# Fetching an adjacency matrix in pairs of row blocks: 4 MB transfers in place of 2 MB ones, and larger x transfers

## The chip, the cores and the metric

The kernel runs on one core of a Trainium2 chip. The metric is the device time of one execution in microseconds. Before the change the median of three runs is 235.88 us (235.42 to 236.04).

## What is computed

One layer of a graph attention network, a residual and a layer norm. The reference, cut to what matters:

```python
ht  = (x @ W).reshape(N, 4, 512).transpose(1, 0, 2)        # x: 4096 x 512, W: 512 x 2048
src = einsum('hnd,hd->hn', ht, a[:, :512, 0]); dst = einsum('hnd,hd->hn', ht, a[:, 512:, 0])
e   = leaky_relu(src[:, :, None] + dst[:, None, :], 0.01) + adj[None]   # adj: 4096 x 4096
att = softmax(e, axis=-1)
y   = einsum('hij,hjd->hid', att, ht).mean(axis=0)
out = layernorm(x + y, axis=-1)
```

The entries of `adj` are 0 or of the order of up to 1e9. In such a row the softmax is one-hot at the largest entry of the row of `adj`, as long as the gap to the second largest is big enough. The kernel relies on this: it finds the column of the largest entry of each row, gathers that row of x, multiplies it by the mean of W over the heads, adds x and normalises. A bound on the attention scores tells whether a row's gap is big enough; a general path behind a branch serves rows for which it isn't. With these inputs the branch isn't taken.

## The kernel before

Partition p of the 128 holds rows 32p to 32p + 31 of x, adj and the output. Block ib (0 to 31) is row 32p + ib of every partition: 128 rows of adj, 16 KB each, 2 MB in all. So for one partition the rows of block ib and ib + 1 lie next to each other in memory. All of x (8 MB) passes through one tile `hold` of 32 slots of 512 columns; the 4 MB of W lie in its slots 16 to 31 at first, until they are used up, and the results are written over x.

One loop over t = 0 to 31 (from L423 on) records the instructions of all engines; each engine then runs its own instructions in that order. In step t:

- **SP** issues all plain transfers, in order: first x, if `x_at` has an entry for t (four blocks each, for blocks 4 to 23, issued at t = 3, 7, 11, 15 and 19), then adj of block t + 5 (`load_adj`, L117). `adj_pool` has six buffers, so the transfer of block ib waits until block ib - 6 has been read. Transfers that SP and ACT issue share eight completion semaphores in turn, so a transfer also waits for the one eight before it.
- **DVE** reduces block t in two halves to the maximum of each segment of its row (L169; segments of 16 columns up to block 17, of 32 from 18 on). Between the halves it handles block t - 2: the second largest entry in the leading segment (L208) and the place of the largest (L214), for which that segment (`lead`) must have been gathered. After the halves it finds the eight largest segments (L176) and their index (L178). At t = 16 come the norms of the attention vectors (`head_norms`, L363): DVE copies and squares `pv`, PE multiplies by ones (L368, tile `px`), DVE and ACT finish.
- **POOL** adds the first index (L185) and gathers the leading segment of block t (L191), and for block t - 2 the column (L216) and then the row of x (L202, tile `y`, four buffers). Every second step it also computes the reciprocal deviations of two blocks (`rstd`, L270) from sums that ACT has made.
- **PE** transposes a head of W (L350, t = 1 to 14), transposes y of block t - 3 (`turn`, L229), adds x by an identity matmul (L237), makes the attention vectors (L358, t = 1 to 14) and multiplies y by the mean of W (`products`, L244).
- **ACT** copies the transposes (L352, L231), takes sums of block t - 4 (L266, L268), the squares of x (L251), and finishes two blocks every second step (L277).

Blocks 28 to 30 arrive in two transfers each and block 31 in four (`pieces`, L114), so that DVE can start on a part. Block 0 has four as well. The results of blocks 24 to 27 wait in a buffer of `adj_pool` (`put_by`, L253). After the loop come the stores, the column search in the whole row of block 31 (L222), its gather, its products in two halves (L286) and the last store.

Of the kernel before, what the change touches and what calls it, by code (L numbers as in the profile page):

```python
# [9 lines left out]
F32 = mybir.dt.float32  # L10
# [10 lines left out]
P = 128  # L21
# [47 lines left out]
def leading_rows(ctx, tc, x, adj, W, a, out, ident, v, n_bad, any_bad):  # L69
# [8 lines left out]
    nc = tc.nc  # L78
    N, D = x.shape
    H = a.shape[0]  # L80
    KB, NB, S = D // P, N // P, N // E
    S_EARLY = N // E_EARLY
    AHEAD = 5
    Q = 4
    PIECES = 4
    LATE = NB - Q
    BEHIND = LATE - Q

    once = ctx.enter_context(tc.tile_pool(name="once", bufs=1))
    adj_pool = ctx.enter_context(tc.tile_pool(name="adj_pool", bufs=AHEAD + 1))  # L90
    y_pool = ctx.enter_context(tc.tile_pool(name="y_pool", bufs=4))
    lead_pool = ctx.enter_context(tc.tile_pool(name="lead_pool", bufs=2 * Q + 1))
    small = ctx.enter_context(tc.tile_pool(name="small", bufs=5))
    rows = ctx.enter_context(tc.tile_pool(name="rows", bufs=2))
    psum = ctx.enter_context(tc.tile_pool(name="psum", bufs=4, space=bass.MemoryType.PSUM))

    adj_rows = adj.rearrange("(p nb) m -> nb p m", nb=NB)
    adj_segs = adj.rearrange("n (s e) -> (n s) e", e=E)
    adj_segs_early = adj.rearrange("n (s e) -> (n s) e", e=E_EARLY)
    x_rows = x.rearrange("(p nb) d -> p nb d", nb=NB)  # L100
# [7 lines left out]
    w_sum = once.tile([P, KB, D], F32, name="w_sum")  # L108
    a_rows = once.tile([2 * H, D], F32, name="a_rows")

    once.tile([P, 32], F32, name="pad_end")
    adj_t = {}

    def pieces(ib):  # L114
        return PIECES if ib in (0, NB - 1) else 2 if ib >= LATE else 1

    def load_adj(ib):  # L117
        if 0 <= ib < NB:
            t = adj_t[ib] = adj_pool.tile([P, N], F32, name="adj_t")
            n = pieces(ib)  # L120
            for k in range(n):
                nc.sync.dma_start(t[:, ts(k, N // n)], adj_rows[ib][:, ts(k, N // n)])

    def load_x(lo, n):
        nc.sync.dma_start(hold[:, ds(lo, n), :], x_rows[:, ds(lo, n), :])
# [7 lines left out]
    for kb in range(KB):  # L133
        load_w(kb)
        load_adj(kb + 1)
    load_x(0, Q)
    for ib in range(KB + 1, AHEAD):
        load_adj(ib)

    make_identity(nc, ident)  # L140
    first = once.tile([P, NB], U32, name="first")
# [18 lines left out]
    seg_of, at_of, lead_of, y_t, yt_of, o_ps = {}, {}, {}, {}, {}, {}  # L160

    def segment_maxima(ib, lo, hi):

        e = E_EARLY if ib < EARLY else E
        if lo == 0:
            seg_of[ib] = small.tile([P, N // e], F32, name=f"seg{e}", bufs=2)
        n = max(pieces(ib), 2)
        for k in range(lo * n // PIECES, hi * n // PIECES):
            nc.vector.tensor_reduce(  # L169
                seg_of[ib][:, ts(k, N // e // n)],  # L170
                adj_t[ib][:, ts(k, N // n)].rearrange("p (s e) -> p s e", e=e), axis=AX.X, op=OP.max,
            )

    def find_segment(ib):
        seg = seg_of.pop(ib)
        nc.vector.max(out=top[:, ib, :], in_=seg)  # L176
        at = at_of[ib] = small.tile([P, 8], U32, name="at")
        nc.vector.max_index(at, top[:, ib, :], seg)  # L178
        if ib < NB - 1:
            fetch_segment(ib)  # L180
# [29 lines left out]
    def find_column(ib):  # L210
        if ib < BEHIND:
            find_inner(ib)
        within = small.tile([P, 8], U32, name="within")
        nc.vector.max_index(within, top[:, ib, :], lead_of[ib])  # L214
        col = small.tile([P, 1], U32, name="col")
        nc.gpsimd.tensor_tensor(col, at_of.pop(ib), within[:, 0:1], op=OP.add)  # L216
        gather_rows(ib, col)
# [15 lines left out]
    def residual(ib):  # L233
        start = ib not in o_ps
        if start:
            o_ps[ib] = psum.tile([P, D], F32, name="o")
        nc.tensor.matmul(o_ps[ib], ident, hold[:, ib, :], start=start, stop=False)  # L237
# [11 lines left out]
    def row_norm(ib):  # L249
        sq = rows.tile([P, D], F32, name="sq")  # L250
        nc.scalar.activation(sq, hold[:, ib, :], AF.Square, accum_out=xx[:, ib : ib + 1])  # L251

    def put_by(ib):  # L253

        if ib == BEHIND:
            o_ps["by"] = adj_pool.tile([P, N // D, D], F32, name="adj_t")
        nc.scalar.copy(o_ps["by"][:, ib - BEHIND, :], o_ps.pop(ib))

    def add_x(engine, ib):
# [10 lines left out]
    def rstd(i):  # L270
        nc.gpsimd.tensor_scalar(sd[:, i], sd[:, i], 1.0 / D, EPS, op0=OP.mult, op1=OP.add)
        nc.gpsimd.tensor_tensor(sd[:, i], sd[:, i], power[:, : i.stop - i.start], op=OP.pow)  # L272
        nc.gpsimd.tensor_mul(nm[:, i], nm[:, i], sd[:, i])
# [57 lines left out]
    def mean_of_heads(kb):  # L331
        o = psum.tile([P, D], F32, name="o")
        for h in range(H):
            nc.tensor.matmul(o, ident, hold[:, w_at + kb * H + h, :], start=(h == 0), stop=(h == H - 1))  # L334
        nc.scalar.activation(w_sum[:, kb, :], o, AF.Copy, scale=1.0 / H)  # L335
# [5 lines left out]
    def turn_a():  # L341
        tp = psum.tile([P, KB, P], F32, name="tp", bufs=2)
        for k in range(KB):
            nc.tensor.transpose(tp[:, k, : 2 * H], a_rows[:, ts(k, P)], ident[: 2 * H, : 2 * H])
        nc.scalar.copy(at_d, tp[:, :, : 2 * H])

    def turn_w(kb, h):
        tp = psum.tile([P, KB, P], F32, name="tp", bufs=2)
        for k in range(KB):
            nc.tensor.transpose(tp[:, k, :], hold[:, w_at + kb * H + h, ts(k, P)], ident)  # L350
        wt = rows.tile([P, KB, P], F32, name="wt")
        nc.scalar.copy(wt, tp)  # L352
        return wt

    def head_vector(kb, h, wt):

        for k in range(KB):
            nc.tensor.matmul(  # L358
                pv[:, kb, h : 2 * H : H], wt[:, k, :], at_d[:, k, h : 2 * H : H],
                start=(k == 0), stop=(k == KB - 1),  # L360
            )

    def head_norms():  # L363
        nc.vector.tensor_copy(v, pv)
        vv = once.tile([P, KB, 2 * H], F32, name="vv")
        nc.vector.tensor_mul(vv, v, v)
        pn = psum.tile([P, KB, 2 * H], F32, name="px", bufs=1)
        nc.tensor.matmul(pn, ones, vv, start=True, stop=True)  # L368
        n2 = once.tile([P, 2 * H], F32, name="n2")
        nc.vector.tensor_reduce(n2, pn.rearrange("p k c -> p c k"), axis=AX.X, op=OP.add)  # L370
        nc.scalar.activation(n2, n2, AF.Sqrt)
        both = once.tile([P, H], F32, name="both")
        nc.vector.tensor_add(both, n2[:, :H], n2[:, H:])
        nc.vector.tensor_reduce(vn, both, axis=AX.X, op=OP.max)
# [40 lines left out]
        nc.vector.tensor_reduce(total, pg, axis=AX.X, op=OP.add)  # L415
        nc.vector.tensor_scalar(any_bad, total, -1.0, float(N), op0=OP.mult, op1=OP.add)

    x_at = {lo - 1: (lo, Q) for lo in range(Q, BEHIND, Q)}
    vectors = [(kb, h) for kb in range(KB) for h in range(H)]
    vectors_at = {t: 2 if t < 3 else 1 for t in range(1, 15)}  # L420
    COLUMN, PROJECT, STATS, FINISH = 2, 3, 4, 6
# [1 line left out]
    for t in range(NB):  # L423
        if t == NB // 2:
            tc.mark_branch_hint_location("general", engines=HINTED)
        if t in x_at:
            load_x(*x_at[t])
        if t + AHEAD == NB - 1:
            load_x(LATE, Q)
        load_adj(t + AHEAD)  # L430
        middle = 1 if t == NB - 1 else 2
        segment_maxima(t, 0, middle)
        if t >= COLUMN:
            find_column(t - COLUMN)
        segment_maxima(t, middle, PIECES)
        pair = FINISH <= t < BEHIND + FINISH and t % 2 == 0
        if pair:
            rstd(slice(t - FINISH, t - FINISH + 2))
        if t == NB - 1:
            for ib in (BEHIND, BEHIND + 2):  # L440
                load_x(ib, 2)
        find_segment(t)
        if t < 2:
            mean_of_heads(t)
        elif t == 2:
            mean_of_heads(2)
            mean_of_heads(3)
        if t == 0:
            turn_a()
        turned = [(*vectors[0], turn_w(*vectors.pop(0))) for _ in range(vectors_at.get(t, 0))]  # L450
        if t == 16:
            head_norms()
        ib = t - PROJECT
        if t == NB - 1:
            for late in range(LATE, NB):
                row_norm(late)
        if t == NB - 2:
            residual(LATE)
            residual(LATE + 1)
        if ib >= 0:  # L460
            turn(ib)
            if ib > BEHIND:
                products(ib - 1, KB - 1, KB)
            if ib < BEHIND:
                residual(ib)
        for some in turned:
            head_vector(*some)
        if ib >= 0:
            products(ib, 0, KB if ib < BEHIND else KB - 1)
        if t >= BEHIND + STATS:  # L470
            put_by(t - STATS)
        elif t >= STATS:
            stats(t - STATS)
            row_norm(t - STATS)
        if pair:
            finish(t - FINISH)
            finish(t - FINISH + 1)
# [218 lines left out]
```

## Time and profile before

| | before |
|---|---|
| median of three runs | 235.88 us (235.42 to 236.04) |
| the profiled execution, its own time | 236.22 us |
| its span, first to last instruction | 234.7 us |
| mean granted TensorE clock | 0.959 |
| busy: PE, DVE, ACT, POOL | 200.7, 192.2, 111.7, 100.7 us |
| bytes moved | 97.06 MB at a mean of 414 GB/s |
| SP's queue (q1) | 10080 packets, 88.08 MB, 89.0% of the 16 engines' span |
| POOL's queue (q0), the gathers | 3584 packets, 8.77 MB, 9.5% |
| DVE idle in front of L169, waiting for adj | 29.4 us in 15 waits |

The 40 digits of an engine's row are its busy share in 40 equal slices of the span, in tenths. In a timeline each line has the start and the length in microseconds, the engine, the line of the kernel, the operation with its tiles and shapes, and in brackets the engine's idle time before it and what ended that. A DMA engine moves packets; the trace records the size, the start and the duration of each. What an SP transfer waits for is not idle time of any engine: it matters only if the DMA engines run out of work.

### The profile page before, as it was taken

To read this page: it belongs to the slowest core of one execution; us is meant where nothing else is said; L and a number is where in the kernel's file an instruction comes from. 1 tells how busy PE (TensorE), PEld (TensorE's weight loads), DVE (VectorE), ACT (ScalarE), POOL (GpSimd) and SP (SyncE) were. 2 spreads that over 40 slices of the span, in tenths; PEclk is the share of its full clock that TensorE was granted. 3 is DMA by queue.
4 is the path that set the end of the run, shared out by engine and by line. 5 is a ranking of instruction groups with operands and counts; after the bars stand their busy time and mean duration, and the time that the engine had idled before them with its cause. 6 is when DMAs were issued, how large, how long until landed. Compare 5 with 4: busy or idle time off the path is not lost.

```text
span 234.7 us, 2494 instructions
## 1 busy us (share of the span) xinstructions
PE 200.7 (86%) x683; PEld 103.0 (44%) x683; DVE 192.2 (82%) x302; ACT 111.7 (48%) x267; POOL 100.7 (43%) x212
## 2 busy tenths in 40 slices
PE   0099859999999999999969979789987988999980
PEld 0034514765656555555525424244433442444360
DVE  2726975669969996999689998998699999989871
ACT  2002112255574647474747464646464555187561
POOL 2022142414626463546444555564364554457400
PEclk9999877999999999999997999979997999999998
DMA  6999999999999999999999999999999999999994
GB/s 233 423 409 430 431 429 415 430 426 425 431 431 421 426 428 428 438 418 436 421 437 431 419 434 422 434 417 435 422 436 413 422 426 423 413 425 420 414 374 197
DMA packets 13697, 97.06 MB, mean 414 GB/s; under 512 B 2152, under 2 KB 2664, under 8 KB 7792
## 3 DMA queue, kind: packets, MB, share of 16 engines
q1 hardware_dynamic: 10080, 88.08, 89.0%
q0 software_dynamic: 3584, 8.77, 9.5%
q8 instruction: 6, 0.10, 0.2%
q14 instruction: 11, 0.09, 0.1%
q10 hardware_dynamic: 16, 0.02, 0.0%
HBM read 88.47 MB, written 8.39 MB: 413 GB/s over the span
## 4 chain that ended last, share of the span: by engine, by line
DMA 48%; POOL 19%; issue 17%; DVE 11%; PE 2%; ACT 0%; POOLq 0%; SPq 0%; DVEq 0%
DMA adj_t<-in_adj_dram 42%; DVE seg L169 8%; POOL y L202 6%; POOL lead L191 5%; DMA y<-in_x_dram,col 3%; DMA lead<-in_adj_dram,row 2%; POOL sd L272 2%; PE o L286 2%; DVE col L222 1%; POOL row L185 1%; POOL start L198 1%; POOL col L216 1%; POOL lead_early L191 1%; DVE at L178 1%; DVE top L176 1%
## 5 line engine op out<-in xcount | busy, mean ns | idle before, releaser
L169 DVE TENSOR_REDUCE seg<-adj_t 128x128 f32<-128x2048 f32 (+3 forms) x68 | 145.9, 2148 | 29.5 <-DMA adj_t<-in_adj_dram 29.4
L244 PE MATMUL o<-w_sum,yt 128*128 128x512 f32 x248 | 116.8, 612 | 0.7 <-ACT yt L231 0.7
L244 PEld LDWEIGHTS o<-w_sum,yt 128*128 128x128 f32 x248 | 45.6, 195 | 55.7 <-issue 44.4
L231 ACT COPY yt<-tp 128x512 f32<-128x512 f32 x32 | 18.8, 588 | 44.4 <-PE tp L229 44.3
L202 POOL DMA_INDIRECT y<-in_x_dram,col x32 | 30.9, 964 | 16.5 <-POOL col L216 15.8
L334 PE MATMUL o<-hold,ident 128*128 128x512 f32 x32 | 21.1, 822 | 15.1 <-POOL row L185 11.5
L237 PE MATMUL o<-hold,ident 128*128 128x512 f32 x52 | 29.0, 645 | 0.0
L229 PE MATMUL tp<-ident,y 128*128 128x128 f32 x128 | 20.0, 280 | 9.2 <-DMA y<-in_x_dram,col 9.1
L185 POOL TENSOR_TENSOR row<-at,first 128x1 uint32<-128x1 uint32 x32 | 6.1, 190 | 43.9 <-DVE at L178 43.6
L229 PEld LDWEIGHTS tp<-ident,y 128*128 128x128 f32 x128 | 14.8, 142 | 21.9 <-issue 20.3
L352 ACT COPY wt<-tp 128x512 f32<-128x512 f32 x16 | 9.2, 587 | 31.5 <-PE tp L350 31.5
L191 POOL DMA_INDIRECT lead_early<-in_adj_dram,row x18 | 18.2, 1010 | 8.8 <-POOL row L185 8.8
L216 POOL TENSOR_TENSOR col<-start,within 128x1 uint32<-128x1 uint32 x31 | 5.9, 189 | 36.5 <-DVE within L214 36.5
L251 ACT ACTIVATE sq<-hold 128x512 f32<-128x512 f32 x32 | 19.8, 619 | 0.0
L358 PEld LDWEIGHTS pv<-at_d,wt 128*128 128x128 f32 x128 | 16.3, 191 | 6.8 <-ACT wt L352 3.7
L334 PEld LDWEIGHTS o<-hold,ident 128*128 128x128 f32 x32 | 8.0, 260 | 25.7 <-POOL row L185 11.5
L335 ACT ACTIVATE w_sum<-o 128x512 f32<-128x512 f32 x4 | 2.4, 598 | 33.6 <-PE o L334 33.6
L277 ACT ACTIVATE hold<-o,nm,sd 128x512 f32<-128x512 f32 x24 | 17.2, 771 | 0.0
L191 POOL DMA_INDIRECT lead<-in_adj_dram,row x14 | 14.1, 1006 | 6.9 <-POOL row L185 6.9
L268 ACT ACTIVATE sq<-o,nm 128x512 f32<-128x512 f32 x24 | 16.5, 688 | 0.8
L358 PE MATMUL pv<-at_d,wt 128*128 128x2 f32 x128 | 15.3, 244 | 0.6 <-ACT wt L352 0.6
L266 ACT ACTIVATE sq<-o 128x512 f32<-128x512 f32 x24 | 14.6, 608 | 0.0
(91 smaller groups left out, 151.4 us busy)
## 6 DMA issues: line engine op xcount, KB each, us to landing
adj_t<-in_adj_dram SPq DMA_DIRECT2D x27, 2048.0 KB
hold<-in_x_dram SPq DMA_DIRECT2D x7, 1024.0 KB
adj_t<-in_adj_dram SPq DMA_DIRECT2D x6, 1024.0 KB
out_dram<-hold SPq DMA_DIRECT2D x10, 512.0 KB
adj_t<-in_adj_dram SPq DMA_DIRECT2D x8, 512.0 KB
hold<-in_L_gnn_W_dram SPq DMA_DIRECT2D x4, 1024.0 KB
out_dram<-hold SPq DMA_DIRECT2D x2, 1024.0 KB
hold<-in_x_dram SPq DMA_DIRECT2D x2, 512.0 KB
```

The costliest lines, as they stand in the source:

```text
L169: nc.vector.tensor_reduce(seg_of[ib][:, ts(k, N // e // n)], adj_t[ib][:, ts(k, N // n)].rearrange("p (s e) -> p s e", e=e), axis=AX.X, op ...
L191: nc.gpsimd.indirect_dma_start(out=lead, out_offset=None, in_=adj_segs_early if early else adj_segs, in_offset=bass.IndirectOffsetOnAxis(a ...
L202: nc.gpsimd.indirect_dma_start(out=y, out_offset=None, in_=x, in_offset=bass.IndirectOffsetOnAxis(ap=col[:, :1], axis=0),)
L229: nc.tensor.transpose(tp[:, kb, :], y[:, ts(kb, P)], ident)
L231: nc.scalar.copy(yt, tp)
L237: nc.tensor.matmul(o_ps[ib], ident, hold[:, ib, :], start=start, stop=False)
L244: nc.tensor.matmul(o_ps[ib], yt_of[ib][:, kb, :], w_sum[:, kb, :], start=(start and kb == 0), stop=(kb == KB - 1),)
L251: nc.scalar.activation(sq, hold[:, ib, :], AF.Square, accum_out=xx[:, ib : ib + 1])
L268: nc.scalar.activation(sq, o, AF.Square, bias=nm[:, i], accum_out=sd[:, i])
L277: nc.scalar.activation(hold[:, ib, :], o_ps.pop(ib), AF.Identity, bias=nm[:, i], scale=sd[:, i])
L334: nc.tensor.matmul(o, ident, hold[:, w_at + kb * H + h, :], start=(h == 0), stop=(h == H - 1))
L358: nc.tensor.matmul(pv[:, kb, h : 2 * H : H], wt[:, k, :], at_d[:, k, h : 2 * H : H], start=(k == 0), stop=(k == KB - 1),)
```

## The change

- The six buffers of `adj_pool` become one tile `ring` of six slots; block ib goes to slot ib mod 6.
- Blocks 4 to 15 are fetched two at a time, 32 KB a partition, by `load_pair`. Pair 4, 5 is issued ahead of the loop, behind x of blocks 0 to 3 (before, block 4 was issued ahead of that x and block 5 at t = 0). Pairs 6, 7 to 14, 15 are issued at t = 2, 4, 6, 8 and 10. Since a pair has one completion, its first block can be read when both have landed. A pair is issued when the second of its two slots is free.
- Block 0 comes in one transfer. DVE reduces it in two halves in place of four quarters.
- x of blocks 4 to 11 comes in one transfer at t = 3, and x of blocks 16 to 23 in one at t = 15. Blocks 12 to 15 keep their own at t = 11. So x of blocks 8 to 11 is now issued ahead of adj of blocks 8 to 11, and x of blocks 20 to 23 ahead of adj of blocks 20 to 23; before, each was issued behind them.
- All other instructions of PE, DVE, ACT and POOL, and their order, are the same. SP issues 59 transfers in place of 70.

```diff
+    SLOTS = AHEAD + 1
+    PAIRED = range(4, 16)
...
-    adj_pool = ctx.enter_context(tc.tile_pool(name="adj_pool", bufs=AHEAD + 1))
...
+    adj_pairs = adj.rearrange("(p nb) m -> p nb m", nb=NB)
...
+    ring = once.tile([P, SLOTS, N], F32, name="adj_t")
...
     def pieces(ib):
-        return PIECES if ib in (0, NB - 1) else 2 if ib >= LATE else 1
+        return PIECES if ib == NB - 1 else 2 if ib >= LATE else 1
+
+    def load_pair(ib):
+        slot = ib % SLOTS
+        for k in range(2):
+            adj_t[ib + k] = ring[:, slot + k, :]
+        nc.sync.dma_start(ring[:, ds(slot, 2), :], adj_pairs[:, ds(ib, 2), :])
 
     def load_adj(ib):
-        if 0 <= ib < NB:
-            t = adj_t[ib] = adj_pool.tile([P, N], F32, name="adj_t")
+        if 0 <= ib < NB and ib not in PAIRED:
+            t = adj_t[ib] = ring[:, ib % SLOTS, :]
...
     load_x(0, Q)
-    for ib in range(KB + 1, AHEAD):
-        load_adj(ib)
+    load_pair(PAIRED[0])
...
-            o_ps["by"] = adj_pool.tile([P, N // D, D], F32, name="adj_t")
+            o_ps["by"] = ring[:, (ib + 2) % SLOTS, :].rearrange("p (b d) -> p b d", d=D)
...
-    x_at = {lo - 1: (lo, Q) for lo in range(Q, BEHIND, Q)}
+    x_at = {Q - 1: (Q, 2 * Q), 3 * Q - 1: (3 * Q, Q), 4 * Q - 1: (4 * Q, 2 * Q)}
...
-        load_adj(t + AHEAD)
+        if t + AHEAD in PAIRED[2:]:
+            if t % 2 == 0:
+                load_pair(t + AHEAD - 1)
+        else:
+            load_adj(t + AHEAD)
```

## The prediction

> **What bounds the kernel now.** I read the page's 40 slices first, then the timelines of DVE, PE and POOL. From the page:
>
> ```profile
> DVE  2726975669969996999689998998699999989871
> ...
> DMA  6999999999999999999999999999999999999994
> GB/s 233 423 409 430 431 429 415 430 426 425 431 431 421 426 428 428 438 418 436 421 437 431 419 434 422 434 417 435 422 436 413 422 426 423 413 425 420 414 374 197
> ```
>
> The 16 DMA engines are never idle between 3 and 224 us. More transfers in flight therefore buy nothing. What the change can still give is a lower DMA cost per byte; what it can lose is the date at which a consumer gets its block. DVE is nearly full as well. Its timeline, first reduction of a block, with the idle time before it in brackets (blocks 8, 9, 12, 16, 17, 20, 24, 27, 31):
>
> ```profile
> 67.56 2.29 DVE L169 TENSOR_REDUCE seg<-adj_t 128x128 f32<-128x2048 f32 x1 [1.67 <-DMA adj_t<-in_adj_dram]
> ...
> 73.28 2.29 DVE L169 TENSOR_REDUCE seg<-adj_t 128x128 f32<-128x2048 f32 x1
> ...
> 92.12 2.29 DVE L169 TENSOR_REDUCE seg<-adj_t 128x128 f32<-128x2048 f32 x1 [1.76 <-DMA adj_t<-in_adj_dram]
> ...
> 116.68 2.29 DVE L169 TENSOR_REDUCE seg<-adj_t 128x128 f32<-128x2048 f32 x1 [1.82 <-DMA adj_t<-in_adj_dram]
> ...
> 124.06 2.28 DVE L169 TENSOR_REDUCE seg<-adj_t 128x128 f32<-128x2048 f32 x1
> ...
> 141.37 2.29 DVE L169 TENSOR_REDUCE seg<-adj_t 128x64 f32<-128x2048 f32 x1 [0.78 <-DMA adj_t<-in_adj_dram]
> ...
> 166.18 2.29 DVE L169 TENSOR_REDUCE seg<-adj_t 128x64 f32<-128x2048 f32 x1 [2.56 <-DMA adj_t<-in_adj_dram]
> ...
> 182.84 2.29 DVE L169 TENSOR_REDUCE seg<-adj_t 128x64 f32<-128x2048 f32 x1 [0.30 <-DMA adj_t<-in_adj_dram]
> ```
>
> Two things are to be seen. Without a wait a block costs DVE 5.67 us (segments of 16) or about 5.4 us (segments of 32), and a block arrives every 5.5 us, every fourth one 2.8 us later, behind an x transfer. And after block 8 all of DVE's waits for adj together are 1.76 + 1.82 + 0.78 + 0.07 + 0.16 + 2.56 + 0.30 = 7.45 us. That is all the delay DVE can make good before the end; from block 27 to block 31 (204.20) it runs without a wait, so a delay left there moves the end.
>
> PE is the second full engine. From turn(0) to turn(11) it repeats every 6.06 us with hardly a gap, and the gather of y decides when it may start. POOL's gather of block 6, PE's turn of it, two later turns, and PE's matmul for the head norms:
>
> ```profile
> 70.89 0.97 POOL L202 DMA_INDIRECT y<-in_x_dram,col  x1 [0.54 <-POOL col L216]
> ```
> ```profile
> 79.77 0.63 PE L229 MATMUL tp<-ident,y 128*128 128x128 f32 x4 [0.17 <-DMA y<-in_x_dram,col]
> ```
> ```profile
> 97.98 0.60 PE L229 MATMUL tp<-ident,y 128*128 128x128 f32 x4
> ...
> 104.04 0.60 PE L229 MATMUL tp<-ident,y 128*128 128x128 f32 x4
> ```
> ```profile
> 122.90 0.38 PE L368 MATMUL px<-vv,ones 128*128 128x32 f32 x2 [2.21 <-DVE vv L366]
> ```
>
> At 122.90 PE waits for DVE; if PE came later, DVE would wait for PE, since the next DVE instructions read px.
>
> **The change, part by part.** All sums are made against the profiled execution: 236.22 us, span 234.7, 0.34 above the median of 235.88.
>
> *DMA work removed.* In the trace's packet records one packet of 16384 bytes takes 611 ns, of 8192 309, of 4096 159, of 4 (a completion) 9. So 8192 bytes cost 302 and a packet about 7. The changed transfers are contiguous on both sides. Pairs: 1536 packets of 16 KB become 768 of 32 KB, 768 x 7 / 16 engines = 0.34 us. Block 0: 4 x 159 become 611, 128 rows, 0.20 us. x: 512 packets of 8 KB become 256, 0.11 us. Eleven transfers fewer, each 16 completions: 0.10 us. Together 0.75 us, and 0 at worst. This is all the change can win, and only if the end still follows the landings.
>
> SP issues eleven transfers less (0.33 to 0.45 us each); SP's queue is 7 to 11 MB ahead of the engines until 170 us (bytes issued less bytes in packets that have ended), so this is worth nothing. A pair is issued when its second slot is free, one block later than before: 5.67 us or 2.4 MB off that lead, still over 5 MB. I cost it at nothing; with the lead gone it would be 5 us of idle DMA.
>
> [...]
>
> *Block 0 in one transfer.* DVE began on its first piece at 4.43 and now begins when 2 MB are there, about 8.5; it would end about 13.5 instead of 10.17. Block 1 is waited for until 16.25 (5.12 us of wait), which hides it. The gather of block 0 goes out at about 15 instead of 12.1 and is needed at 26.
>
> *Pairs and the earlier x.* Both blocks of a pair are usable when the second has landed. Block 4 moves from 39.28 to about 48.5 (block 5 was there at 48.80); blocks 4 to 7 then take 4 x 5.67 and end at 71.2. Pair 8, 9: block 8 landed for 67.56, block 9 5.4 us later (73.0; DVE took it unwaited at 73.28), and now x of blocks 8 to 11 (1 MB, 2.7 us) goes ahead of it: 75.7, less 0.3 saved so far, 75.4. So block 8 starts 7.85 us later than before. DVE's remaining slack was 7.45 us. With no further wait DVE would come out 0.4 us late at block 31. Later pairs land before DVE is ready for them (10, 11 at about 86.2 against 86.7); x of blocks 20 to 23 is also early, but DVE is then over 4 us behind.
>
> *The gathers.* This cost is not in the trace of before, since no packet there is over 16 KB. What is there: y gathers that PE waited for took, from issue to PE's turn, 8.88, 8.24, 8.55, 8.43, 7.88 us while the SP queue moved 16 KB packets (blocks 6, 16, 18, 21, 22), and 6.74, 7.69, 7.07, 7.34 near the end, with 4 and 8 KB packets (blocks 26, 27, 29, 31). Medians 8.43 and 7.2: doubling 8 KB to 16 KB costs a gather 1.2 us. Doubling again adds twice as many bytes, 2.4 us. Bounds: 0, if a 32 KB row still moves as 16 KB packets, and 5 x 0.604 = 3.0, if each of the four data packets of an engine and its completion wait for one longer packet. I take 2.4, from the rows.
>
> [...]
>
> Now PE. The gather of block 6 is issued 3.3 us after block 8 starts (67.56 to 70.89): 78.7. turn(6) follows at 78.7 + 8.43 + 2.4 = 89.5 (79.77 before). From there PE has no slack: five periods of 6.06 to turn(11), 5.62 to turn(12) (110.10 to 115.72), 4.8 to the end of its products: PE reaches px at 130.2. DVE, left alone, starts block 16 at 120.9 (75.4 + 49.12 - 3.58 of waits between 67.56 and 116.68) and wants px at 127.1, as 116.68 to 122.90 shows. It must wait 3.1 us. From px to block 17 were 1.16 us, so block 17 starts at 131.4 instead of 124.06, 7.3 late. Slack left after it: 0.78 + 0.07 + 0.16 + 2.56 + 0.30 = 3.87. Block 31 starts about 3.5 us late.
>
> *The tail.* From 204.20 to the end the order is unchanged: the column search, y of block 31 (issued 216.13, PE 223.47), its products, the last store. All of it follows DVE. The gather may be faster, as fewer stores are in flight: 7.34 against the fastest 6.74, so 0 to 0.6; I take 0.2.
>
> Sum: 236.22 + 3.5 - 0.2 = 239.5 profiled; less 0.34, **239.2 us** as a median.
>
> **Rivals.** *The gathers are not slowed* (32 KB moved as 16 KB packets, or the queue not alternating). For it: no trace shows a packet over 16 KB. Against: 4, 8 and 16 KB rows each moved as one packet. Then turn(6) is at 87.1, PE at px at 127.8, block 17 at 129.0, 4.9 late, less 3.87: 1.07 late, 0.2 of it lost in the tail: 237.1 profiled, 236.7 as a median. By DVE alone (block 17 at 120.9 + 7.38 = 128.3) it would be 236.1.
>
> *Faster: the landings decide the end again.* If DVE has caught up by block 27, block 27 lands 0.75 us earlier than 182.84 and everything behind it follows: 235.1. It decides as soon as DVE's delay at block 17 is below 3.1 us (3.87 - 0.75), that is block 17 starts before 127.2. For it: DMA is the chain's largest part, and 7.85 against 7.45 is close. Against: PE alone brings block 17 to 129.0.
>
> *Worse: DVE also waits for leads.* The small gather needs its answer 7.12 us after issue (104.32 to DVE's search at 111.44). With 4 and 8 KB packets it took 5.56 and 5.98 (205.06 to 210.62, 199.73 to 205.71). One data packet and one completion each behind a 32 KB packet would add 2 x 0.9 us: 7.4 to 7.8, a wait of 0.3 to 0.7 in each of blocks 10 to 15. About 3 us of that lie under DVE's wait for px; what is over, and the row gathers that POOL then issues late, would cost 1 to 2 more: 240.2 to 241.4.
>
> **How the numbers follow.** Forecast 0.52 (own range 237.6 to 240.2), gathers not slowed 0.22, faster 0.13, worse 0.13. The range reaches from 235.5 to 241.4; it leaves out most of the faster case and a little at the top. A difference of 0.3% (0.7 us) is about what a measurement of this kernel can tell from no change. Slower by more: forecast, worse, and the upper part of the first rival, 0.71; within: 0.16; faster: 0.13.
>
> **What would show it.** In the changed kernel's trace: packets of 32768 bytes near 1.21 us; block 4 starting near 48.5 and block 8 near 75.4, with a DVE wait before each; PE's turn of block 6 near 89.5 behind a wait for y; no PE idle time before px, and a DVE wait of about 3 us behind it; block 17 near 131.4; no DVE wait for adj after block 8; block 31 near 207.7. Wrong would be: x landing behind pair 8, 9; DVE idle for adj after block 17 (then the delay was made good); gathers no slower between 45 and 107 us; idle DMA engines before 200 us.

## The result, and the profile after

Six runs of the changed kernel have a median of 246.31 us (245.08 to 248.87), six of the kernel before 235.56 (235.36 to 236.04). The ratio of the means is 1.0449 with a 95% interval of 1.0391 to 1.0506; the run at 248.87 us, over 1.5% above the fastest, is left out of it, and the median of the other five is 245.23 us. The profiled execution took 245.21 us with a span of 243.7, at a granted clock of 0.954 (0.959 before). So the change costs about 10 us (10.75 by the medians, 9.0 by the two profiled executions): the direction was forecast, the size was not, and the time lies above the range.

The page of the changed kernel, in the rows that were shown of the kernel before (40 slices, busy share in tenths):

```profile
DVE  0666790199945965679999899999999999989882
DMA  6999999999999999999999999999999999998225
GB/s 247 430 430 418 430 461 427 432 430 432 431 435 422 434 428 427 404 429 432 429 419 431 433 432 416 435 427 424 424 421 424 429 415 424 420 414 339 90 107 201
```

DVE now has a weak stretch from slice 12 to 18 (67 to 110 us: digits 4, 5, 9, 6, 5, 6, 7), and the DMA engines run out of work three slices before the end. The loss was made early; at the end the data were there and the engines were late.

DVE's waits in the changed kernel (waited for; us in total, times, longest):

```profile
DVE seg L177 <- DMA adj_t<-in_adj_dram: 25.6, 5, 11.7
DVE inner L216 <- DMA lead_early<-in_adj_dram,row: 14.2, 5, 3.6
```

The second line is new. Before, the list had only 0.7 us of waiting for a lead, for two late ones (`lead`, L214), and none for `lead_early`. The five waits in DVE's timeline, each with the first reduction of the next block:

```profile
70.75 0.18 DVE L216 MAX8 inner<-lead_early 128x8 f32<-128x16 f32 x1 [3.65 <-DMA lead_early<-in_adj_dram,row]
...
74.64 2.27 DVE L177 TENSOR_REDUCE seg<-adj_t 128x128 f32<-128x2048 f32 x1
...
79.32 0.18 DVE L216 MAX8 inner<-lead_early 128x8 f32<-128x16 f32 x1 [2.41 <-DMA lead_early<-in_adj_dram,row]
...
82.81 2.27 DVE L177 TENSOR_REDUCE seg<-adj_t 128x128 f32<-128x2048 f32 x1
...
87.20 0.18 DVE L216 MAX8 inner<-lead_early 128x8 f32<-128x16 f32 x1 [2.12 <-DMA lead_early<-in_adj_dram,row]
...
90.69 2.27 DVE L177 TENSOR_REDUCE seg<-adj_t 128x128 f32<-128x2048 f32 x1
...
95.55 0.18 DVE L216 MAX8 inner<-lead_early 128x8 f32<-128x16 f32 x1 [2.59 <-DMA lead_early<-in_adj_dram,row]
...
99.03 2.27 DVE L177 TENSOR_REDUCE seg<-adj_t 128x128 f32<-128x2048 f32 x1
...
104.67 0.18 DVE L216 MAX8 inner<-lead_early 128x8 f32<-128x16 f32 x1 [3.37 <-DMA lead_early<-in_adj_dram,row]
...
108.16 2.27 DVE L177 TENSOR_REDUCE seg<-adj_t 128x128 f32<-128x2048 f32 x1
```

Blocks 8 to 12 start at 74.64, 82.81, 90.69, 99.03 and 108.16: 7.9 to 9.1 us apart, where DVE's own work is 5.67. POOL's gathers of this stretch in the changed kernel:

```profile
71.88 0.97 POOL L210 DMA_INDIRECT y<-in_x_dram,col  x1 [0.54 <-POOL col L224]
...
75.92 0.96 POOL L199 DMA_INDIRECT lead_early<-in_adj_dram,row  x1 [0.92 <-POOL row L193]
...
80.45 0.96 POOL L210 DMA_INDIRECT y<-in_x_dram,col  x1 [0.54 <-POOL col L224]
...
83.69 1.07 POOL L199 DMA_INDIRECT lead_early<-in_adj_dram,row  x1 [0.52 <-POOL row L193]
...
88.33 0.96 POOL L210 DMA_INDIRECT y<-in_x_dram,col  x1 [0.54 <-POOL col L224]
...
91.55 0.96 POOL L199 DMA_INDIRECT lead_early<-in_adj_dram,row  x1 [0.51 <-POOL row L193]
```

The lead issued at 75.92 is used at 87.20 (11.3 us), the one issued at 91.55 at 104.67 (13.1 us); 7.12 was what DVE could spare. The y gathers are as late. PE's turns of blocks 5, 6 and 7 in the changed kernel, whose gathers went out at 71.88, 80.45 and 88.33:

```profile
84.83 1.09 PE L237 MATMUL tp<-ident,y 128*128 128x128 f32 x4 [2.26 <-DMA y<-in_x_dram,col]
...
94.41 0.63 PE L237 MATMUL tp<-ident,y 128*128 128x128 f32 x4 [1.73 <-DMA y<-in_x_dram,col]
...
102.31 0.63 PE L237 MATMUL tp<-ident,y 128*128 128x128 f32 x4 [1.65 <-DMA y<-in_x_dram,col]
```

That is 12.95, 13.96 and 13.98 us from issue to use, 8.43 in the median before and 10.83 by the prediction.

The trace's packet records say why. Pairs do move as packets of 32768 bytes: 768, median 1213 ns. POOL's queue carries 3584 packets, 7 for each block on each of the 16 engines (3584 / 32 / 16): four of y, one of the lead and two completions. Between 62 and 102 us it moved 556 of them on 16 engines, 0.87 per engine and microsecond, so one POOL packet in 1.15 us, while SP's queue started 485 large ones: a little over one POOL packet for each. Seven of them take 8.06 us, DVE's new step.

That the step has this length proves nothing by itself, since POOL issues seven packets for each block, however long a block takes. What shows that the queue sets the pace is that it never ran empty: from 62 to 102 us no two of its packets, over all engines, started more than 0.67 us apart. In the kernel before it stood still at four places in the same stretch, for 0.9 to 2.9 us (once from 72.77 to 75.03). Counted in the order of issue, from the first packet's start to the last one's end (gathers issued from 54 to 96 us), a y gather took 3.5 us in the median before and a lead 1.4, together 4.9 of DVE's 5.67; now they take 5.5 and 2.4, together 7.9. So the leads queue up behind the y gathers of earlier blocks.

How it adds up, by starts of blocks on DVE (us):

| | block 4 | 8 | 12 | 17 | 24 | 31 | time |
|---|---|---|---|---|---|---|---|
| before | 39.28 | 67.56 | 92.12 | 124.06 | 166.18 | 204.20 | 236.22 |
| after | 47.91 | 74.64 | 108.16 | 138.16 | 177.05 | 214.65 | 245.21 |

Block 8 is 7.08 us late. From there to block 17 DVE waits 2.41 + 2.12 + 2.59 + 3.37 = 10.49 us for leads and saves the 1.76 + 1.82 = 3.58 us that it waited for adj before: 6.91 more, 14.0 in all, and 14.10 is measured. Of these 3.87 are made good behind block 17 (the slack of the prediction): 10.2, and block 31 is 10.45 late. The tail then takes 1.45 us less (29.05 against 30.5 us from block 31 to the span's end): 9.0, the difference of the two profiled executions. Its last gather is 3.7 us shorter, since the DMA engines are nearly idle by then, but little of that counts: its last packet ended at 229.72 and PE took the rows at 233.18, without a wait, because it was still at the products of earlier blocks. That is 0.74 us sooner after block 31's start than before; the last store gives the other 0.7.

### The profile page after: what moved, and what is told of

Read it like the earlier page. It is cut to its first block, busy times and chain, and to the rows that moved or that the text cites. A ratio compares the mean times of both kernels' runs of the same rounds, so it can differ in the third digit from the quotient of the medians.

```text
span 243.7 us, 2474 instructions
## 1 busy us (share of the span) xinstructions
PE 201.7 (83%) x683; PEld 104.0 (43%) x683; DVE 191.2 (78%) x300; ACT 112.1 (46%) x267; POOL 100.6 (41%) x212
## 3 DMA queue, kind: packets, MB, share of 16 engines
q0 software_dynamic: 3584, 8.77, 9.3%
## 4 chain that ended last, share of the span: by engine, by line
DMA 28%; POOL 23%; issue 23%; PE 19%; DVE 3%; ACT 2%; POOLq 0%; SPq 0%
DMA adj_t<-in_adj_dram 15%; PE o L252 12%; DMA y<-in_x_dram,col 9%; POOL y L210 7%; POOL lead L199 4%; DMA hold<-in_L_gnn_W_dram 4%; POOL lead_early L199 4%; POOL sd L280 3%; PE tp L237 2%; DVE seg L177 2%; PE o L245 2%; POOL start L206 2%; POOL row L193 2%; POOL col L224 2%; PE o L294 1%
## 5 line engine op out<-in xcount | busy, mean ns | idle before, releaser
L177 DVE TENSOR_REDUCE seg<-adj_t 128x128 f32<-128x2048 f32 (+2 forms) x66 | 145.1, 2204 | 25.6 <-DMA adj_t<-in_adj_dram 25.6
L252 PEld LDWEIGHTS o<-w_sum,yt 128*128 128x128 f32 x248 | 44.9, 193 | 54.2 <-issue 44.0
L237 PE MATMUL tp<-ident,y 128*128 128x128 f32 x128 | 20.7, 286 | 20.5 <-DMA y<-in_x_dram,col 20.2
L342 PE MATMUL o<-hold,ident 128*128 128x512 f32 x32 | 20.8, 809 | 14.7 <-DMA hold<-in_L_gnn_W_dram 14.7
L245 PE MATMUL o<-hold,ident 128*128 128x512 f32 x52 | 28.2, 629 | 0.0
L366 PEld LDWEIGHTS pv<-at_d,wt 128*128 128x128 f32 x128 | 17.7, 205 | 7.9 <-issue 4.1
L199 POOL DMA_INDIRECT lead<-in_adj_dram,row x14 | 14.1, 1005 | 6.9 <-POOL row L193 6.6
L366 PE MATMUL pv<-at_d,wt 128*128 128x2 f32 x128 | 16.4, 252 | 0.6 <-ACT wt L360 0.6
## 6 DMA issues: line engine op xcount, KB each, us to landing
adj_t<-in_adj_dram SPq DMA_DIRECT2D x16, 2048.0 KB, 13.9
```

The source lines that it names most:

```text
L177: nc.vector.tensor_reduce(seg_of[ib][:, ts(k, N // e // n)], adj_t[ib][:, ts(k, N // n)].rearrange("p (s e) -> p s e", e=e), axis=AX.X, op ...
L199: nc.gpsimd.indirect_dma_start(out=lead, out_offset=None, in_=adj_segs_early if early else adj_segs, in_offset=bass.IndirectOffsetOnAxis(a ...
L237: nc.tensor.transpose(tp[:, kb, :], y[:, ts(kb, P)], ident)
L252: nc.tensor.matmul(o_ps[ib], yt_of[ib][:, kb, :], w_sum[:, kb, :], start=(start and kb == 0), stop=(kb == KB - 1),)
L366: nc.tensor.matmul(pv[:, kb, h : 2 * H : H], wt[:, k, :], at_d[:, k, h : 2 * H : H], start=(k == 0), stop=(k == KB - 1),)
```

## The experiments

The experiments ask three things: is it the size of the packets, and not the joint completion, the order of x or the ring; does the queue of POOL carry the loss; and is there a version that gains. The theory is that 32 KB packets slow POOL's queue below the rate at which DVE feeds it. Its rivals are the joint landing of a pair, the earlier x, and PE as the bound. Each kernel is compared with the kernel before on the same chip.

### Packets of 16 KB in the same pairs

**e1_apart** moves the slots of the ring 8 elements apart, so that the two rows of a pair are no longer one run in the tile; **e11_apart_512** moves them 128 elements apart. Both keep the pairs, their single completion and all order.

```diff
-    ring = once.tile([P, SLOTS, N], F32, name="adj_t")
+    ring = once.tile([P, SLOTS, N + 8], F32, name="adj_t")[:, :, :N]     # e11: N + 128
```

> The changed kernel, but the six slots of the ring lie 32 bytes apart in each partition, so that a pair is still one transfer with one completion while each row of it moves as a packet of 16 KB. Theory 'gather queue': in the changed kernel each of the seven packets per engine that POOL's queue has for a block (four of y, one of lead, two completions) waits for one SP packet of 1.21 us, 8.5 to 9.2 us a block against DVE's 5.67, so DVE waits 14.2 us for leads. With 16 KB packets a block's gathers take about 5 us again: leads land 5 to 6.5 us after issue, no DVE wait for leads over 1 us in total, block 17 starts at 128 to 130, time 236 to 238. Rival 'pair landing' (the pair's one completion and late slot release cost the time): DVE as late as in the changed kernel, block 17 at about 138, time 244 to 247.

Measured: 239.16 us, ratio 1.0154 (1.0135 to 1.0174), above the 236 to 238 expected. The list has no wait for `lead_early` (1.5 us in all for later leads), and block 12 starts at 97.91 in place of 108.16, so about two thirds of the loss (246.31 - 239.16 of 10.75 us) went with the packet size. But the 16 KB packets took 625 ns in the mean where those of the kernel before took 612, so e1 also has a slower DMA. Therefore the wider spacing:

> The changed kernel with slots 512 bytes apart in place of the 32 bytes of the first run with slots apart. That run's packets of 16 KB took 625 ns on the mean against 612 before, so part of its 3.7 us may be a slower DMA that the 32 bytes made and not the pairs. Theory: with 512 bytes the packets take 611 to 615 ns, block 17 starts at 128 to 130, 4 to 6 us late, of which DVE makes good 3.9: 236 to 237.6. Rival 'the pairs' landing costs 3.7 us': 239 again.

Measured: 237.06 us (235.52 to 238.43, 11 runs), ratio 1.0057 (1.0031 to 1.0083), packets of 614 ns. DVE's waits in e11:

```profile
DVE n L378 <- PE px L376: 2.4, 1, 2.4
...
DVE inner L216 <- DMA lead_early<-in_adj_dram,row: 0.7, 2, 0.4
```

And DVE at blocks 8 and 17 in e11:

```profile
74.14 2.29 DVE L177 TENSOR_REDUCE seg<-adj_t 128x128 f32<-128x2048 f32 x1 [3.65 <-DMA adj_t<-in_adj_dram]
```
```profile
128.74 0.19 DVE L378 TENSOR_REDUCE n<-px 128x8 f32<-128x32 f32 x1 [2.40 <-PE px L376]
...
129.50 2.28 DVE L177 TENSOR_REDUCE seg<-adj_t 128x128 f32<-128x2048 f32 x1
```

This is the first rival of the prediction, "the gathers are not slowed", in nearly every date: block 8 at 74.14 behind a wait for its pair, PE's turn of block 6 at 87.66 (87.1 forecast), block 17 at 129.50 (129.0 forecast), 237.06 us (236.7 forecast). Only the wait for px, 2.40 us, is longer than by that rival's dates (127.8 - 127.1 = 0.7): DVE was there 1.1 us sooner (block 16 at 119.81 in place of 120.9), PE half a microsecond later. With the same pairs and half the packet size, 246.31 - 237.06 = 9.25 of the 10.75 us are gone (245.21 - 237.35 = 7.9 of 9.0 by the profiled executions). POOL's queue keeps up again: a y gather takes 3.7 us and a lead 1.6 by the same count, together 5.3. What remains, about 1.5 us, is the rest of the change, the joint landing with it.

### The order of x, and the parts without pairs

**e2_x_as_before** is the changed kernel with x in its old order; **e5_apart_x_before** the same on e1; **e3_no_pairs** is the kernel before with only block 0 in one transfer and x in larger ones.

```diff
-    x_at = {Q - 1: (Q, 2 * Q), 3 * Q - 1: (3 * Q, Q), 4 * Q - 1: (4 * Q, 2 * Q)}
+    x_at = {lo - 1: (lo, Q) for lo in range(Q, BEHIND, Q)}
```

> The changed kernel with x of blocks 4 to 23 fetched four blocks at a time, as before the change; pairs and block 0 as in the changed kernel. Theory 'gather queue': the 32 KB packets stay, so the leads still take 9 to 12 us and DVE's waits for them stay over 10 us; block 8 starts about 2.7 us earlier: 243 to 246. Rival 'x order' (x ahead of adj makes DVE late): most of the loss goes, 236 to 239.

> The changed kernel with slots 32 bytes apart (16 KB packets) and x of blocks 4 to 23 in four-block transfers as before: only the joint completion of pairs and block 0's single transfer are left. The run with slots apart left 3.7 us over the kernel before, block 8 there started 7.7 us late (75.25 against 67.56). Theory 'delay that DVE cannot make good': here block 8 starts at about 72.5, 5 us late, which is inside the 7.45 us of slack: block 17 before 127.5, time 235.3 to 237. Rival 'the joint completion itself costs, whatever the x order': 238.5 to 240, as with slots apart.

> The kernel before with block 0 in one transfer and x of blocks 4 to 11 and 16 to 23 in one each, but no pairs. Theory 'gather queue': no packet over 16 KB, no DVE wait for leads; DMA work 0.3 us shorter; blocks 8 to 11 come 2.7 us late once, which DVE's slack of 7.45 us covers: 235 to 236. Rival 'x order': 238 or more.

Measured: e2 244.0 us, ratio 1.0326 (1.0262 to 1.0389). The waits for leads are still there:

```profile
DVE inner L216 <- DMA lead_early<-in_adj_dram,row: 12.2, 4, 3.8
```

e3 235.64, ratio 0.9998 (0.9982 to 1.0014): block 0 and the larger x transfers cost and give nothing alone. e5 239.11, ratio 1.0145 (1.013 to 1.0159), a miss: 235.3 to 237 was expected. Its DVE waits for adj again at blocks 24, 27 and 31:

```profile
DVE seg L177 <- DMA adj_t<-in_adj_dram: 31.7, 13, 10.5
```

So there the landings are late: its 16 KB packets took 623.9 ns, 12 more than before, as in e1. With slots 32 bytes apart the order of x makes no difference (239.11 against 239.16). The x order is not the cause; at most it adds about 2 to 3 us on top of the pairs (246.31 against 244.0, with wide spreads of 245.08 to 248.12 and 241.96 to 245.34).

### One pair as two transfers, and fewer pairs

**e6_two_transfers** issues both blocks of a pair in the same step, but as two transfers of 2 MB with a completion each. **e7_two_pairs** and **e12_four_pairs** have only the first two or four of the six pairs.

```diff
-        nc.sync.dma_start(ring[:, ds(slot, 2), :], adj_pairs[:, ds(ib, 2), :])
+        for k in range(2):
+            nc.sync.dma_start(ring[:, slot + k, :], adj_rows[ib + k])
```
```diff
-    PAIRED = range(4, 16)
+    PAIRED = range(4, 8)        # e12: range(4, 12)
```

> The changed kernel with each pair issued at the same place as two transfers of 2 MB, each with its own completion; ring, issue order, slot release of pairs and x as in the changed kernel. Theory 'gather queue and joint landing': packets are 16 KB and a block can be read when it has landed, so block 4 starts near 41 to 43, block 8 near 70.5 (x of blocks 8 to 11 ahead of it), no lead waits over 1 us, 235.3 to 236.5. Rival 'late issue of pairs' (SP issues a block later than before, and behind waits for a second slot): 238 or more.

> The changed kernel with only blocks 4 to 7 in pairs (two transfers of 4 MB), the others alone; x and block 0 as in the changed kernel. Theory 'gather queue': 32 KB packets move only until about 56 us; the gathers slowed by them fall in the time in which DVE waits for block 4 or for block 8, block 8 starts near 70.5, and nothing is left at the end: 235.3 to 237. Rival 'any pair costs about a sixth of the 10.75 us': 239.

> The changed kernel with blocks 4 to 11 in pairs (four pairs) and the others alone. 32 KB packets move until about 84 us in place of 104. Theory 'gather queue': about half of the five DVE waits for leads (14.2 us) are left, those before 85 us: block 17 near 132 to 134, time 239 to 242; two pairs gave 237.24, six 246.31. Rival 'the loss comes from what is late in blocks 4 to 8, whatever follows': near 237.2, as with two pairs.

Measured: e6 235.78, ratio 1.0008 (0.9996 to 1.0019). The ring, the issue in steps of two, block 0 and x together are worth nothing either way, and the joint completion costs 237.06 - 235.78, about 1.3 us (e11's runs alone spread over 2.9). It is not a run without waits: 3.4 us for leads, where under 1 was expected, and block 17 at 127.71, 3.65 late, inside the slack of 3.87. The larger of the two lead waits follows a late issue, not a slow queue:

```profile
DVE inner L217 <- DMA lead_early<-in_adj_dram,row: 3.4, 2, 2.3
```
```profile
100.76 0.19 POOL L280 TENSOR_SCALAR sd<-sd 128x2 f32<-128x2 f32 x1 [3.99 <-ACT sq L277]
...
102.55 1.07 POOL L200 DMA_INDIRECT lead_early<-in_adj_dram,row  x1 [0.37 <-POOL row L194]
```

e7 237.24, ratio 1.0067 (1.0054 to 1.008), slightly above what was expected; e12 239.51 (237.16 to 239.91), ratio 1.0133 (1.0094 to 1.0171). The lead waits of e7, and then of e12:

```profile
DVE inner L216 <- DMA lead_early<-in_adj_dram,row: 4.3, 6, 2.5
```
```profile
DVE inner L216 <- DMA lead_early<-in_adj_dram,row: 6.9, 4, 3.7
```

No pairs (e3), two, four and six give 235.64, 237.24, 239.51 and 246.31 us, and 0.2, 4.3, 6.9 and 14.2 us of waits for early leads. Block 17 starts 1.2, 5.9, 8.2 and 14.1 us late, so from two pairs on the slack of 3.87 us is used up and covers nothing more. The last step is the largest, because the changed kernel's waits at 87.20, 95.55 and 104.67 (8.1 us together) fall in the time of the last two pairs: the last of e12's large packets starts at 82.4 us, that of the changed kernel at 103.4. Of e12's waits 6.3 us, at 70.56 and 79.38, lie before that. e7's waits have another source, as in e6: they come from 78.92 to 123.13 us, long after its last large packet (55.7). POOL waits 13.9 us for ACT's sums there (2.8 in the changed kernel) and, as it works in order, issues leads late. So only e12 and the changed kernel tell about the queue. Why the sums come late in e7 was not tested.

### Fewer gather packets beside the same 32 KB packets

**e4_quarter_y** is the changed kernel with y gathers of 128 columns in place of 512; **e8_before_quarter_y** the same edit on the kernel before, as its control.

```diff
+    x_quarters = x.rearrange("n (s e) -> (n s) e", e=P)
...
-        y = y_t[ib] = y_pool.tile([P, D], F32, name="y")
+        y = y_t[ib] = y_pool.tile([P, P], F32, name="y")
...
-            out=y, out_offset=None, in_=x,
+            out=y, out_offset=None, in_=x_quarters,
...
-            nc.tensor.transpose(tp[:, kb, :], y[:, ts(kb, P)], ident)
+            nc.tensor.transpose(tp[:, kb, :], y, ident)
```

The index still counts whole rows, so these are quarters of other rows than the kernel needs; the two runs tell about sizes and dates alone.

> The changed kernel, but each y gather fetches 128 columns of a row of x in place of 512, and the four transposes read these same columns (three quarters of each gathered row are left out). A y gather is then one packet of 4 KB per engine in place of four, and a block has four packets per engine on POOL's queue in place of seven. Theory 'gather queue' (the queue's throughput): 4 x 1.25 = 5.0 us a block, below DVE's 5.67, so DVE's waits for leads fall from 14.2 us to under 3, block 17 starts before 132, time 235 to 239. Rival 'lead latency' (a lead is slow by its own two packets, as the prediction had it): leads are as late as in the changed kernel, time 243 to 246.

> The kernel before with y gathers of 128 columns (three quarters of each gathered row are left out), as the control for the changed kernel with quarter y gathers, which ran in 231.8: both move 6.3 MB less. Theory 'gather queue': before, the queue was not the limit, so the gain is the bytes alone, at most 6.3 MB / 427 GB/s = 14.7 us and less where DVE's 5.4 to 5.7 us a block bounds: 226 to 231. The part of the changed kernel's loss that is left beside it is then that of the landings, 1 to 4 us.

Measured: e4 231.78, ratio 0.9838 (0.9797 to 0.988); e8 226.21, ratio 0.9584 (0.9562 to 0.9606). POOL's queue now has 2048 packets, 4 for each block and engine: 4 x 1.15 = 4.6 us by estimate, and by the count above a y gather took 2.6 us and a lead 2.5, together 5.1, less than DVE's 5.67. DVE's waits for early leads in e4 fall from 14.2 us to 0.8:

```profile
DVE inner L217 <- DMA lead_early<-in_adj_dram,row: 0.8, 2, 0.5
```

Issue to last completion of a lead between 54 and 100 us: 4.9 to 6.3 us in the kernel before, 6.1 to 12.6 in the changed one (five of seven above 9), about 6 to 7.2 in e4. So a lead by itself is little slowed by 32 KB packets; what holds it is the gather packets in front of it. The loss by pairs with quarter rows is 231.78 - 226.21 = 5.6 us in place of 10.75 (4.7 by the profiled executions). These 4.7 are in place by block 17 already (125.11 against 120.43) and stay. At block 17 e11 is about as late (129.50 against 124.06, 5.4 us). That the loss here is more than e11's 1.5 comes from the end: nothing is made good, as from block 17 to 31 both kernels take 75.67 us. This pair of runs changes the bytes moved too (6.3 MB less), so it supports the mechanism and does not give its share.

### The lead ahead of the y gather

**e13_lead_first** turns the order on POOL: the lead of block t goes out ahead of y of block t - 2. **e14_before_lead_first** is the control.

```diff
-            find_column(t - COLUMN)
+            col = find_column(t - COLUMN, gather=False)
...
         find_segment(t)
+        if t >= COLUMN:
+            gather_rows(t - COLUMN, col)
```

> The changed kernel with POOL's order in a step turned round: the gather of the leading segment of block t goes out first, then the y gather of block t - 2, which is some 3 us later than before. Same gathers, same bytes, same 32 KB packets. If a lead is late only because the y gather issued 3.2 us before it stands ahead of it in POOL's queue ('order'), a lead now has 5 us or more behind the last y gather: leads land in 7 to 8 us, DVE waits for them for under 5 us in all, block 17 starts before 134, 238 to 242. If the queue cannot carry seven packets per engine in one of DVE's steps ('throughput', 7 x 1.15 us = 8.1 us against 5.67), the y gathers pile up and the leads stand behind them all the same: DVE still takes about 8 us a block while 32 KB packets move, its waits for leads stay over 10 us, 244 to 248.

> The control: the kernel before with the same turned order. With 16 KB packets seven packets take about 5.1 us, so both theories expect no DVE wait for leads; PE gets each y 3 us later, for which it has time except near the end: 235.5 to 238.

Measured: e13 271.68, ratio 1.1535 (1.1516 to 1.1554); e14 260.71, ratio 1.107 (1.0999 to 1.114). Both missed, and the control as much as the other, so this pair doesn't test what it was made for. Where e14's time goes is in POOL's waits and its timeline:

```profile
POOL sd L273 <- ACT sq L270: 64.2, 13, 7.1
```
```profile
82.76 0.19 POOL L216 TENSOR_TENSOR col<-start,within 128x1 uint32<-128x1 uint32 x1 [1.57 <-DVE within L214]
87.67 0.19 POOL L273 TENSOR_SCALAR sd<-sd 128x2 f32<-128x2 f32 x1 [4.72 <-ACT sq L270]
...
89.45 1.06 POOL L191 DMA_INDIRECT lead_early<-in_adj_dram,row  x1 [0.37 <-POOL row L185]
...
90.91 0.96 POOL L202 DMA_INDIRECT y<-in_x_dram,col  x1 [0.16 <-issue]
```

The column is known at 82.76. Its y gather must now wait behind POOL's reciprocal deviations (87.67, 4.72 us of waiting for ACT) and the next lead, and goes out at 90.91, 8 us later. ACT's sums depend on PE's products, these on y, and y on POOL: a circle in which each step waits for the one before. That the difference between the two, 11.0 us, is that of the changed kernel and the one before is no evidence, since both run at another pace.

### Is there something to win at the end?

In the changed kernel the y gather of block 31 found the queues nearly empty: issued at 226.67, landed 3.05 us later, where it took 6.7 us beside SP's stores. **e9_hold_14** and **e10_hold_18** are the kernel before with its last stores in another order, so that the last gather could meet an emptier queue.

```diff
-    for ib in range(2 * Q, BEHIND, 2):
+    for ib in range(2 * Q, 14, 2):        # e10: 18
...
-    for ib, n in ((NB - 4, 1), (NB - 3, 1), (BEHIND, 2), (BEHIND + 2, 2), (NB - 2, 1)):
+    for ib, n in ((NB - 4, 1), *((ib, 2) for ib in range(14, BEHIND, 2)), (NB - 3, 1), (BEHIND, 2), (BEHIND + 2, 2), (NB - 2, 1)):
```

> The kernel before, with the store of block 28 (ready at about 218 us) moved ahead of the stores of blocks 14 to 23 in SP's order, so that SP issues nothing between about 206 and 218 us and the queue has run empty when the row of x for block 31 is gathered. In the changed kernel that gather, with an empty queue, took 3.05 us from issue to landing against 6.7 before. Theory: it lands 2.5 to 3.5 us earlier, and the five held stores (2.5 MB, 6 us) still end before the last one: 232.5 to 234.5. Rival 'the held stores end last': 235.5 to 238.

> The same with the store of block 28 moved ahead of the stores of blocks 18 to 23 only: SP stops at about 209 us with 4 MB to go, so that the queue is empty only from about 218 on. Theory: the gather of block 31 gains 1 to 2.5 us and the held 1.5 MB end in time: 233 to 235. Rival: 235.5 to 237.

Measured: 235.5, ratio 0.9998 (0.9986 to 1.001), and 235.47, ratio 0.9999 (0.9987 to 1.0011). Neither gains. SP's queue still held about 0.6 and 1.6 MB at 217.2, and the DMA engines were busy throughout. In e10 the gather was hardly faster (issued at 215.39, last packet ended at 221.92, 6.5 us). In e9 it was (215.70 to 220.76, 5.1 us in place of 6.7), but PE took the rows only at 222.30, without waiting for them, and from there to the span's end it took 11.7 us in place of 11.2. So the faster gather met a PE that was still busy, as at the end of the changed kernel. No version was found that beats the kernel before; e3, e6, e9 and e10 equal it.

## Why the prediction was right or wrong, point by point

**Right.** Block 4 started at 47.91 (48.5 forecast), and 32 KB rows move as single packets of 1213 ns (1.21 us forecast). No wait for adj came after block 8, and the slack of 3.87 us behind block 17 held: in the changed kernel 14.10 - 3.87 = 10.2 against 10.45 at block 31, and in e12 8.16 - 3.87 = 4.3 against 4.76. Block 0, the issue order of SP and the larger x cost nothing (e3, e6). The loss is where it was looked for, at gathers beside 32 KB packets, and the "worse" rival named the wait that decided.

**Right for another reason.** Block 8 started at 74.64 (75.4 forecast), but the trace shows no wait for adj there. The wait of 3.65 us for a lead at 70.75 took its place: the agreement is luck. In e11, without that wait, the pair's landing starts block 8 at 74.14.

**The step that failed** is the price of the gathers, in two sentences. One is "Doubling again adds twice as many bytes, 2.4 us": the y gathers took 13.0 to 14.0 us, 4.5 to 5.6 more than 8.43, and above the bound of 3.0. The other is "One data packet and one completion each behind a 32 KB packet would add 2 x 0.9 us: 7.4 to 7.8, a wait of 0.3 to 0.7". For a lead alone that is about what e4 shows (6 to 7.2 from issue to landing). But both sentences price one gather on a queue that keeps up, and the queue no longer did. It carries 7 packets per block and engine, each takes 1.15 us beside 32 KB packets, and 8.06 us is more than DVE's 5.67 us step. From there the wait is no latency to be added once: it is the difference of two rates, paid in every block as long as pairs land. So DVE waited 2.1 to 3.7 us in each of blocks 7 to 11, where the "worse" rival had 0.3 to 0.7 in each of blocks 10 to 15 and the forecast none. What was needed for this was at hand (3584 packets, 32 blocks, 16 engines, 1.21 us forecast for a large packet), and the estimate 7 x 1.21 = 8.5 us would have been enough to see it.

That large packets slow a gather at all was an estimate in the prediction, from rows of 4 to 16 KB (8.43 us against 7.2). The trace of the changed kernel shows it: between 62 and 102 us POOL's queue moved one packet per engine in 1.15 us beside packets of 1.213 us, 556 to 485, and a y gather took 5.5 us in place of 3.5 by the count above. The eleven transfers fewer were priced at nothing, and rightly as far as the runs show: e3, with 65 transfers of SP in place of 70, takes the same time (ratio 0.9998).

One reading of the prediction was off, and nothing rests on it: from 10 to 170 us, bytes issued less bytes landed put SP's queue 8 to 13 MB ahead, not 7 to 11. The 0.75 us of DMA time that it hoped to save shows in no run's time.

**The bound at px.** The prediction let DVE wait 3.1 us for PE at px. With leads late DVE itself came last: its wait there is 0.56 us, and block 17 came at 138.16 in place of 131.4. In e11, without the lead waits, the wait for px is there (2.40 us). **The tail** gave 1.45 us instead of 0.2, half of it at the last gather and half at the last store.

**What stays open.** e11 splits the 10.75 us into about 9.25 for the size of the packets and 1.5 for the rest. How the 9.25 divide between leads that queue behind y gathers and PE that comes later because of y isn't separated, as both pass through one queue, and e13 and e14, which should have done it, changed the pace of the whole loop.

## What to carry to other kernels

When a transfer is made larger so that its rows become longer packets, count what else uses the same DMA engines. As an estimate, multiply the packets per step and engine of the other queue by the new packet's time, and compare that with the step. Here 7 x 0.61 = 4.3 us (4.9 measured) and 4 x 1.21 = 4.9 us (5.1 measured in e4) are below DVE's 5.67, and the queue only answered later; 7 x 1.21 = 8.5 us (7.9 measured) is above, and the queue set the pace. That was most of the result here.

## What the runs showed of the hardware that was not expected

- Setting slots of a tile 32 bytes apart made 16 KB packets take 625 ns instead of 612, and cost more than 512 bytes, with 614 ns (ratios 1.0154 and 1.0057). Why isn't known.
- A gather of 128 rows of 2 KB took 3.05 us with nearly no other traffic and 6.7 us at the same place beside SP's stores.
- The granted clock of TensorE fell around two of PE's waits for y. Windows of the changed kernel (us; length; busy and count of PE, PEld, DVE, ACT, POOL; PEclk, DMA share, GB/s); in the kernel before PEclk is 1.00 in both:

```profile
48.00:60.00 12.00, 7.19 (x34) 4.52 (x33) 11.79 (x17) 3.64 (x9) 3.83 (x8) 0.89 1.00 427
60.00:75.00 15.00, 15.00 (x47) 8.57 (x46) 10.69 (x17) 6.96 (x17) 6.24 (x13) 0.75 1.02 438
```

PEclk is 0.50 from 57.39 to 67.63 us and from 84.70 to 88.11. After a wait of 4.81 us, which ended at 59.49, four transposes took 1.09 us, where they take 0.60 at a PEclk of 1.00 (at 97.98 in the kernel before). After a shorter wait, the one of 2.26 us that ended at 84.83 (shown above), they took 1.09 us too. It isn't the cause of the loss, since e11 has the same clock (0.73 from 60 to 75 us).
